# Contexts of block 0 on quadrants of TensorE, a new order for the first two units, and one buffer for what stays

## The chip, the cores and the metric

The kernel runs on one core of one Trainium2 chip. The metric is the device time of one execution in microseconds. Three runs of the kernel before took 1060.54, 1061.24 and 1062.72 us, median 1061.24 us. A further execution was recorded by the hardware profiler: it took 1059.08 us, of which the span from the first to the last instruction is 1057.3 us.

The engines are named as in the profile: PE (TensorE matmul), PEld (TensorE weight load), DVE (VectorE), ACT (ScalarE), POOL (GpSimd) and SP (SyncE, which issues the DMAs here). L12 is line 12 of the kernel before.

## The reference

The input x has 32 sequences of 64 tokens with 512 features, in float32, and each sequence has a condition vector. Two blocks follow one another. Block 0 is a conditioned RMS norm, attention with rotary positions, 8 query heads of 64 and one shared key/value head, and then a gated MLP of width 2048. Block 1 is a conditioned layer norm and an attention with 16 heads of 32, whose 4 key/value heads come from a latent of 128.

```python
def block0(x, pos, cond):                       # 8 query heads of 64, one kv head
    h = ada_rms(x, cond, ln1_w, ln1_tw)         # norm, times w * (1 + cond @ tw.T)
    q, k, v = h @ Wq.T, h @ Wk.T, h @ Wv.T      # split in heads
    q, k = rope(q, pos), rope(k, pos)
    attn = softmax(einsum('bkgsd,bktd->bkgst', q, k) / sqrt(64))
    ctx = einsum('bkgst,bktd->bkgsd', attn, v)  # the contexts that the change touches
    x = x + ctx @ Wo.T
    h = ada_rms(x, cond, ln2_w, ln2_tw)
    return x + (silu(h @ Wg.T) * (h @ Wu.T)) @ Wd.T

def block1(x, cond):                            # 16 query heads of 32, 4 kv heads
    scale, shift = split(cond @ W_ada.T + b_ada)
    h = layernorm(x) * (1 + scale) + shift
    q, c_kv = h @ Wq.T, h @ Wkd.T
    k, v = c_kv @ Wku.T, c_kv @ Wvu.T
    q, k = rope(q), rope(k)
    attn = softmax(masked(q @ k.T / sqrt(32)))
    return x + (attn @ v) @ Wo.T
```

## The kernel before

**Tiling.** The work is cut into 8 units of 256 tokens, that is, 4 sequences each. Features lie on the 128 partitions and tokens in the columns, so x of a unit is a tile of 128 x 4 x 256. For each unit there are three jobs: `attention0` (L569), `mlp` (L961) and `attention1` (L718), each a Python generator that emits a piece of the program and yields. All matmuls are in float32; the profile records each as two matmuls, and two weight loads.

**Attention of block 0.** `query` projects half of the query features into a bank of PSUM and turns them by their angles; `keys_values` does the same for the shared key and value. The values are transposed (`vt`, L643) and copied by ACT into `vblk0` (L646). `vblk0` is block-diagonal: for each sequence it holds 128 x 128, with v of 64 x 64 at top left and again at bottom right, and zeros elsewhere. The zeros are written once by POOL in `early` (L990). The scores (`sc`, L664) are computed on quadrants of the array: heads lie two to a partition tile, one in the upper and one in the lower 64 rows, so each matmul is 64 x 64. After the softmax, each half t of the unit (2 sequences) is transposed in four pieces into one bank (`pp`, L549), copied to `pT` by ACT (L550), and multiplied with the block-diagonal values:

```python
cx = abank(f"cx0_{u}_{t}").rearrange("p (b c s) -> p b c s", b=2, c=KC)
for b in range(2):                      # L681: two matmuls of 128 x 128, 256 columns
    nc.tensor.matmul(cx[:, b], vb[:, 2 * t + b].rearrange("p r d -> p (r d)"),
                     pT[:, :, b * S : (b + 1) * S], start=True, stop=True)
for b in range(2):                      # L690: two copies of 128 x 256 on ACT
    nc.scalar.copy(to[:, b], cx[:, b])
```

The contexts `cT` then go through the output projection (`output`, L553, tile `po`) and are added to x by DVE (L562). The squares of the new x (`sq_b`, ACT L489), their means (`qs_b`, L467), a root with its inverse (`r_b`), its spread over the partitions (`row_b`, L389) and the scaled `h` lead to the MLP.

**MLP.** Each of the three weight matrices is handled with seven products of half-size blocks in place of eight. A set of weights holds three loaded blocks and four sums of blocks. In the first pass the sums are made by DVE and POOL (`combine`, L243 to L246) and kept in DRAM; later passes load all seven. The tiles are `gu` (gate and up, L875) and `down` (L934).

**Order.** Engines work through their queues in order. The order of PE's pieces is set in two ways. In the start, `FIRST` (L48) is a string: letter a takes the next piece of unit 0's attention, b of unit 1's, m of the modulations 1 to 3 (products of the conditions with the modulation weights, tiles `ps_mod` and `pt_mod`). The whole stretch is kept in this order on PE by `ordered` (L96). After it, `Order.run` (L72) chooses between the MLP of a unit, the attention of block 0 of the next and of block 1 of earlier units, by the cost and latency that each piece yields. In the start and the tail `homes["now"]` lets banks be drawn from all of PSUM; in the main stage the attentions have the two banks "at". ACT, DVE, POOL and SP take their instructions as the program emits them. SP's queue holds nearly all loads, in program order: x of unit 0, the weights of the query, x of unit 1, modulation 1, `wo0`, the sets, modulations 2 and 3, and, after `FIRST`, the weights of block 1.

**Buffers.** Tensors that stay (identity, small constants, keys, values, angles, the weights of both attentions) have one tile each (`fixed`, L129). The angles of two units are computed in borrowed tiles, `p0` and `pT0` (L308). The last unit of block 1 borrows `vblk0[0]` for its values, and POOL clears it ahead of the tail (L1059).

Of the kernel before, what the change touches and what calls it, by code (L numbers as in the profile page):

```python
# [10 lines left out]
F32 = mybir.dt.float32  # L11
# [6 lines left out]
P = 128  # L18
B, S, D = 32, 64, 512
T = B * S  # L20
KC = D // P
# [23 lines left out]
TURN = (0.15911865234375, 3.628432750701904e-05, 6.4192136051133275e-09, 1.4247115856860781e-12)  # L45
ROUND = 12582912.0
WARM = 11
FIRST = "aaaaaaa bb a mm aa b a b aa bbb a b aa a bb a mmmm a bbbb".replace(" ", "")  # L48
TWO_PI = float(np.nextafter(np.float32(2 * np.pi), np.float32(0)))


# [56 lines left out]
def two_blocks(ctx: ExitStack, tc: tile.TileContext, a: dict, out: bass.AP):  # L108
# [17 lines left out]
        homes["n"] += 1  # L126
        return bank(tags[homes["n"] % len(tags)], name)

    def fixed(tag, shape, dtype=F32):  # L129
        return const.tile(shape, dtype, tag=tag, name=tag)  # L130

    def work(tag, shape, name, bufs=2):
        return wk.tile(shape, F32, tag=tag, name=name, bufs=bufs)


    ident = fixed("ident", [P, P])
    make_identity(nc, ident)
    ones = fixed("ones", [P, P])
# [6 lines left out]
    spread = fixed("spread", [P, US, P])  # L145
# [7 lines left out]
    eps0 = fixed("eps0", [P, 1])  # L153
    nc.gpsimd.memset(eps0, EPS0)
    eps1 = fixed("eps1", [P, 1])
    nc.gpsimd.memset(eps1, EPS1)
    quarter = fixed("quarter", [P, 1])
    nc.gpsimd.memset(quarter, float(np.float32(np.pi / 2)))

    positions = []  # L160
# [4 lines left out]
        positions.append(t)  # L165

    load_positions(0)
    small = fixed("small", [P, C_ALL])
# [6 lines left out]
    sign_of = small[:, C_SIGN:C_ALL]  # L175


    kblk0 = [fixed(f"kblk0{i}", [P, US, S]) for i in range(2)]

    vblk0 = [fixed(f"vblk0{i}", [P, US, 2, S]) for i in range(2)]  # L180
    vblk1 = [fixed(f"vblk1{i}", [P, US, 2, 2 * HD1]) for i in range(2)]

    s0a = fixed("s0a", [P, KC, B])
    s0b = fixed("s0b", [P, KC, B])
    s1 = fixed("s1", [P, KC, B])
    t1 = fixed("t1", [P, KC, B])
    angle = fixed("angle", [P, 2, NU * S])


    wqkv = [fixed("wqkv0", [P, KC, 384]), fixed("wqkv1", [P, KC, 256])]  # L190
    wo0 = fixed("wo0", [P, KC, D])
    wq1 = fixed("wq1", [P, KC, D])
    wkd = fixed("wkd", [P, KC, LAT])
    wkv1 = fixed("wkv1", [P, 2, P])
    wo1 = fixed("wo1", [P, KC, D])

    x_units = {}

# [109 lines left out]
    def angles(u0):  # L308

        cols = slice(u0 * S, (u0 + 2) * S)  # L310

        def some(tag, name, cols=512, bufs=2):
            return work(tag, [P, cols], f"{name}_{u0}", bufs)[:, : 2 * S]

        posi = positions.pop()
        posf, sign = some("u", "posf"), some("v", "sign")
        both = work("p0", [P, 2, 512], f"ang_lo_{u0}", 1)
        ang, lo = both[:, 0, : 2 * S], both[:, 1, : 2 * S]
        hi, prod = some("pT0", "hi", 512, 1), some("r0", "prod", UT, 1)
# [121 lines left out]
    def tile4(room, tag, name):  # L441
        return space(room, tag, KC * UT, name).rearrange("p (c t) -> p c t", t=UT)
# [126 lines left out]
    def attention0(u, room, early=None, late=None):  # L569
# [71 lines left out]
        vt = abank(f"vt_{u}").rearrange("p (b d) -> p b d", d=P)  # L641
        for b in range(US):
            nc.tensor.transpose(vt[:, b, :HD0], vT[HD0:, b].rearrange("p r s -> p (r s)"), ident[HD0:, HD0:])  # L643
        for i in range(2):
            rows = slice(i * S, (i + 1) * S)
            nc.scalar.copy(vb[rows, :, i, :], vt[rows, :, :HD0])  # L646
        yield 0.3, 4.5


# [23 lines left out]
            yield 0.5 * len(ts), 5.0 * ts[0] if lean else 10.0  # L673

        cT = tile4(room, "h", f"cT0_{u}")
        for t in range(2):
            pT = turned(ps[t], f"0_{u}_{t}", space(room, "pT", 512, f"pT0_{u}_{t}")).rearrange("p (c t) -> p c t", c=KC)
            yield 0.5, 1.2
            cx = abank(f"cx0_{u}_{t}").rearrange("p (b c s) -> p b c s", b=2, c=KC)
            for b in range(2):  # L680
                nc.tensor.matmul(  # L681
                    cx[:, b],
                    vb[:, 2 * t + b].rearrange("p r d -> p (r d)"),
                    pT[:, :, b * S : (b + 1) * S],
                    start=True,
                    stop=True,
                )
            to = cT[:, :, t * P : (t + 1) * P].rearrange("p c (b s) -> p b c s", s=S)
            for b in range(2):
                nc.scalar.copy(to[:, b], cx[:, b])  # L690
            yield 0.9, 1.5 * t
        yield from output(u, cT, wo0, f"0_{u}")


# [361 lines left out]
    def spare(tag, cols, name, bufs=2):  # L1056
        return work(tag, [P, cols], f"own_{name}", bufs)

    nc.gpsimd.memset(vblk0[0], 0.0)  # L1059
    two = [spare("h2", 1024, f"h2{i}") for i in range(2)]  # L1060
    few = spare("cs", 512, "few", 1)
    extra = spare("x", 1024, "kb6", XB)
# [5 lines left out]
        "latT": [few[:, :UT]],  # L1068
        "kr": [few[:, UT:]],
        "kb": [extra[:, :512]],  # L1070
        "pT": [extra[:, 512:], spare("pT0", 512, "pT6", 1)] * 2,
# [98 lines left out]
```

## Time and profile before

| | from | value |
|---|---|---|
| median of three runs | times | 1061.24 us |
| profiled execution | times | 1059.08 us |
| its span, first to last instruction | page | 1057.3 us |
| PE busy | page, part 1 | 1013.2 us (96%) |
| PEld busy | page, part 1 | 944.1 us (89%) |
| DVE, ACT, POOL busy | page, part 1 | 548.6, 324.5, 434.7 us |
| context matmul of block 0 (L681), 64 records | tile `cx` | 379 ns each |
| context copy of block 0 (L690), 32 | tile `cx` | 377 ns each |
| copy of values (L646), 16 | tile `vt` | 367 ns each |

A record of a matmul runs from its first to its last word through the array, so records that follow one another overlap: the distance between the starts of neighbours, not the length of one, is what it takes of PE. A line of the timeline groups such records (x4 is four records, two matmuls). The times in it count from the start of the span. What stands in square brackets is how long the engine was idle ahead of the group and what ended that.

### The profile page before, as it was taken

Reading aid. Unit: us, or ns where it says so; the run is one execution under the profiler, and the core shown is the slowest. Engines: PE = TensorE matmul, PEld = TensorE weight load, DVE = VectorE, ACT = ScalarE, POOL = GpSimd, SP = SyncE. Lnnn points to the kernel's source line nnn. Section 1 sums busy time; section 2 is a strip of 40 time slices with the busy share of each in tenths; the row PEclk is TensorE's granted clock in tenths of the full one; section 3 lists DMA queues with packets and bytes.
Section 4 is the critical chain, followed back from the end, with each engine's and each line's share of the span. In section 5 each row is a group of like instructions: output and inputs, shape, how many; then the busy total and the mean of one; then the engine's idle time right before and its main releaser. Section 6 shows DMA issues by size and latency. Waiting matters only on the chain.

```text
span 1057.3 us, 21448 instructions
## 1 busy us (share of the span) xinstructions
PE 1013.2 (96%) x8538; PEld 944.1 (89%) x8538; DVE 548.6 (52%) x1377; ACT 324.5 (31%) x682; POOL 434.7 (41%) x520
## 2 busy tenths in 40 slices
PE   7889999999999989999999998999999999999887
PEld 6779999998999989999999997999999899999765
DVE  4866646543455485343653268532755335452363
ACT  4333112344124242132422323331423422241132
POOL 4424545344255434254342543324533335432541
PEclk8989999999999999999999999999999999999899
DMA  7916896354556465662646555455735557565001
GB/s 276 328 43 219 294 312 240 136 210 151 203 210 210 143 217 177 227 222 105 224 172 221 184 182 183 150 203 203 251 118 196 173 189 284 197 230 178 11 1 40
DMA packets 68274, 198.53 MB, mean 188 GB/s; under 512 B 7248, under 2 KB 15184, under 8 KB 67792
## 3 DMA queue, kind: packets, MB, share of 16 engines
q1 hardware_dynamic: 68176, 197.17, 53.6%
q8 instruction: 68, 1.11, 0.4%
q14 instruction: 30, 0.25, 0.1%
HBM read 180.37 MB, written 16.78 MB: 186 GB/s over the span
## 4 chain that ended last, share of the span: by engine, by line
PE 79%; DVE 10%; POOL 5%; issue 2%; DMA 2%; ACT 1%; SPq 0%; ACTq 0%; POOLq 0%; DVEq 0%
PE gu L875 32%; PE down L934 16%; PE po L514 10%; PE q L514 9%; PE pp L549 2%; PE lat L514 1%; PE cx L681 1%; PE cx L845 1%; PE sc L821 1%; PE kv L514 1%; DMA set<-in_wmlp 1%; PE sc L664 1%; DVE mx L534 1%; DVE sm L542 1%; DMA x<-in_x 1%
## 5 line engine op out<-in xcount | busy, mean ns | idle before, releaser
L875 PE MATMUL gu<-h,set 128*128 128x128 f32 x2048 | 288.3, 276 | 8.9 <-DVE c L894 5.2
L875 PEld LDWEIGHTS gu<-h,set 128*128 128x128 f32 x2048 | 259.4, 192 | 15.9 <-issue 10.7
L875 PE MATMUL gu<-hc,set 128*128 128x128 f32 x1536 | 215.3, 275 | 0.0
L875 PEld LDWEIGHTS gu<-hc,set 128*128 128x128 f32 x1536 | 193.6, 192 | 0.5
L913 POOL TENSOR_TENSOR act<-c,c 128x384 f32<-128x384 f32 x64 | 66.6, 1040 | 193.6 <-DVE c L901 117.5
L934 PE MATMUL down<-td,set 128*128 128x128 f32 x1024 | 136.4, 276 | 3.2 <-POOL td L916 3.2
L934 PEld LDWEIGHTS down<-td,set 128*128 128x128 f32 x1024 | 125.1, 192 | 4.5 <-POOL td L916 4.2
L887 ACT COPY e<-gu 128x128 f32<-128x128 f32 x128 | 33.7, 265 | 279.1 <-PE gu L875 268.8
L901 DVE TENSOR_TENSOR c<-gu,u 128x256 f32<-128x256 f32 x128 | 53.4, 419 | 118.1 <-PE gu L875 117.8
L514 PE MATMUL po<-cT,wo 128*128 128x256 f32 x480 | 108.4, 380 | 2.4 <-DVE sm L542 2.1
L934 PE MATMUL down<-act,set 128*128 128x128 f32 x768 | 109.2, 278 | 0.0
L889 DVE TENSOR_TENSOR u<-e,gu 128x128 f32<-128x128 f32 x128 | 36.1, 282 | 130.4 <-ACT e L887 129.8
L514 PEld LDWEIGHTS po<-cT,wo 128*128 128x128 f32 x480 | 89.3, 190 | 14.2 <-ACT cT L854 2.6
L934 PEld LDWEIGHTS down<-act,set 128*128 128x128 f32 x768 | 97.9, 192 | 4.2 <-issue 2.4
L544 POOL TENSOR_TENSOR p<-p,sm 128x512 f32<-128x512 f32 x40 | 41.3, 1052 | 116.5 <-DVE sm L543 110.6
L525 POOL TENSOR_TENSOR qT<-u_q,v_q 128x512 f32<-128x512 f32 x30 | 38.1, 1270 | 93.8 <-DVE v_q L524 93.8
L562 DVE TENSOR_TENSOR x<-x,po 128x512 f32<-128x512 f32 x32 | 22.0, 687 | 75.9 <-PE po L514 75.9
L970 ACT ACT_TABLE_LOAD x34 | 43.6, 1283 | 55.8 <-DVE c L901 55.4
L514 PE MATMUL q<-h,wqkv 128*128 128x256 f32 x256 | 58.4, 380 | 0.0
L514 PE MATMUL q<-h,wq 128*128 128x256 f32 x224 | 52.1, 385 | 1.6 <-POOL h L750 1.6
L514 PEld LDWEIGHTS q<-h,wqkv 128*128 128x128 f32 x256 | 47.7, 191 | 6.4 <-issue 0.4
L915 POOL TENSOR_TENSOR td<-act 128x256 f32<-128x256 f32 x64 | 47.6, 744 | 10.0 <-DVE act L912 3.8
(276 smaller groups left out, 1407.4 us busy)
## 6 DMA issues: line engine op xcount, KB each, us to landing
set<-sums SPq DMA_DIRECT2D x168, 512.0 KB, 5.8
set<-in_wmlp SPq DMA_DIRECT2D x192, 384.0 KB, 4.7
sums<-set SPq DMA_DIRECT2D x24, 512.0 KB, 4.7
x<-in_x SPq DMA_DIRECT2D x8, 512.0 KB, 5.7
out_x<-x SPq DMA_DIRECT2D x16, 256.0 KB, 2.1
mod<-in_mod SPq DMA_DIRECT2D x7, 512.0 KB, 6.2
a<-in_wmlp SPq DMA_DIRECT2D x24, 128.0 KB, 4.3
wo<-in_wo SPq DMA_DIRECT2D x2, 1024.0 KB, 8.4
```

Source lines behind the costliest of these rows:

```text
L514: nc.tensor.matmul(ps, w[:, k, cols], h[:, k, :], start=(k == 0), stop=(k == KC - 1))
L525: nc.gpsimd.tensor_tensor(dst, u, v, ALU.add)
L544: nc.gpsimd.tensor_tensor(p8, p8, sm.unsqueeze(2).to_broadcast(wide), ALU.mult)
L562: nc.vector.tensor_tensor(x[:, part], x[:, part], po, ALU.add)
L875: nc.tensor.matmul(ps, w[:, slot, k * P : (k + 1) * P], b[of][:, k], start=start and k == 0, stop=k == 1, skip_group_check=True)
L887: nc.scalar.copy(e, ps[:, 0])
L889: nc.vector.tensor_tensor(u2, e, ps[:, 1], ALU.add)
L901: nc.vector.tensor_tensor(c.rearrange("p (a b) t -> p a b t", b=2)[:, :, 1], ps[:, 2:4], u2.unsqueeze(1).to_broadcast([P, 2, HT]), ALU.add,)
L913: nc.gpsimd.tensor_tensor(act[:, 1:4], gate[:, 1:4], c[:, 1:4], ALU.mult)
L915: nc.gpsimd.tensor_tensor(td[:, 0:2], act[:, 1:3], act[:, 0:2], ALU.subtract)
L934: nc.tensor.matmul(sums_of[u][p][:, c], w[:, slot, c * P : (c + 1) * P], b[of], start=q % NP == 0 and i % 2 == 0 and c == 0, stop=q % NP = ...
L970: nc.scalar.activation(gate[2][:, 0], gate[0][:, 0], AF.Silu)
```

## The change

**Contexts on quadrants.** `vblk0` keeps its 4 x 64 columns of values, once in the upper and once in the lower 64 partitions, with no zeros. A context is now 64 x 64 times 256 columns: row half r by the parity of the head, column half b by the sequence. The results of row half r go to a bank of their own, and ACT copies each quadrant. Units 0 and 1 (the "lean" ones) do this for each half t, with 4 matmuls and 4 copies of 64 x 256; units 2 to 7 do both halves together after both transposes, with 8 matmuls and 4 copies of 64 x 512. The values are copied by one ACT instruction instead of two, and two of the four early memsets fall away. The yields that the planner reads change with it.

**FIRST.** The string of the first two units is another. The pieces on PE up to the first scores are as before. After that the order, with one entry per piece, is:

```
before: q0_1_0 pp_0_0 tab_1,row_1 cx0_0_0 pp_0_1 q0_1_1 cx0_0_1 vt_1 po_0_0 po_0_1 sc0_1_0 sc0_1_1
        qs_b0 ps_mod2 pt_mod2 ps_mod3 pt_mod3 row_b0 pp_1_0 cx0_1_0 pp_1_1 gu cx0_1_1 gu po_1 ...
after:  q0_1_0 tab_1,row_1 pp_0_0 q0_1_1 cx0_0_0 pp_0_1 vt_1 ps_mod2 pt_mod2 cx0_0_1 sc0_1_0 sc0_1_1
        po_0_0 po_0_1 ps_mod3 pp_1_0 qs_b0 cx0_1_0 pt_mod3 pp_1_1 row_b0 cx0_1_1 gu po_1 ...
```

Each modulation piece also issues loads on SP's queue, so that loads of modulation 2 come ahead of `wo0` there, and the sets 3 and 4 behind it.

**Buffers.** All tensors that stay are slices of one tile, "stays", of 14103 columns. The angles have tiles of their own, `ang0` to `ang2`; `pT0` has two buffers; the last unit's values lie in a spare buffer of `pT1`.

```diff
+STAY = 14103
-FIRST = "aaaaaaa bb a mm aa b a b aa bbb a b aa a bb a mmmm a bbbb".replace(" ", "")
+FIRST = "aaaaaaa bb a mm aa bb a bbb aa b mm a bb aa a m b a b m b a b".replace(" ", "")
...
-    def fixed(tag, shape, dtype=F32):
-        return const.tile(shape, dtype, tag=tag, name=tag)
+    stays = {"all": const.tile([P, STAY], F32, tag="stays", name="stays"), "at": 0}
+
+    def fixed(shape):
+        n, i = int(np.prod(shape[1:])), stays["at"]
+        stays["at"] += n
+        assert stays["at"] <= STAY
+        t = stays["all"][:, i : i + n]
...
-    vblk0 = [fixed(f"vblk0{i}", [P, US, 2, S]) for i in range(2)]
+    vblk0 = [fixed([P, US, HD0]) for i in range(2)]
...
-        both = work("p0", [P, 2, 512], f"ang_lo_{u0}", 1)
-        ang, lo = both[:, 0, : 2 * S], both[:, 1, : 2 * S]
-        hi, prod = some("pT0", "hi", 512, 1), some("r0", "prod", UT, 1)
+        ang, lo, hi = (some(f"ang{i}", f"ang{i}", 2 * S, 1) for i in range(3))
+        prod = some("r0", "prod", UT, 1)
...
-    RING = {"h": 2, "p1": 2, "pT1": 2}
+    RING = {"h": 2, "p1": 2, "pT0": 2, "pT1": 2}
...
-        for i in range(2):
-            rows = slice(i * S, (i + 1) * S)
-            nc.scalar.copy(vb[rows, :, i, :], vt[rows, :, :HD0])
+        nc.scalar.copy(vb, vt[:, :, :HD0])
...
+        pTs = []
+
+        def contexts(ts):
+
+            banks = [abank(f"cx0_{u}_{ts[0]}_{r}").rearrange("p (t c s) -> p t c s", t=2, c=KC) for r in range(2)]
+            for i, t in enumerate(ts):
+                for b in range(2):
+                    for r, cx in enumerate(banks):
+                        rows = slice(r * S, (r + 1) * S)
+                        nc.tensor.matmul(
+                            cx[b * HD0 : (b + 1) * HD0, i],
+                            vb[rows, 2 * t + b],
+                            pTs[t][rows, :, b * S : (b + 1) * S],
+                            start=True,
+                            stop=True,
+                        )
+            by_two = cT.rearrange("p c (t b s) -> p t c b s", b=2, s=S)[:, ts[0] : ts[-1] + 1]
+            for r, cx in enumerate(banks):
+                for b in range(2):
+                    nc.scalar.copy(by_two[r * HD0 : (r + 1) * HD0, :, :, b], cx[b * HD0 : (b + 1) * HD0, : len(ts)])
+
         for t in range(2):
...
-            cx = abank(f"cx0_{u}_{t}").rearrange("p (b c s) -> p b c s", b=2, c=KC)
...
-            for b in range(2):
-                nc.scalar.copy(to[:, b], cx[:, b])
-            yield 0.9, 1.5 * t
+            if lean:
+                contexts([t])
+                yield 0.6, 1.5 * t
+        if not lean:
+            contexts([0, 1])
+            yield 1.1, 2.5
...
-        for z in (*vblk0, *vblk1):
+        for z in vblk1:
             nc.gpsimd.memset(z, 0.0)
...
-    nc.gpsimd.memset(vblk0[0], 0.0)
+    zeros = spare("pT1", 512, "vb7", 2).rearrange("p (b r d) -> p b r d", b=US, r=2)
+    nc.gpsimd.memset(zeros, 0.0)
...
-        "vb": vblk0[0],
+        "vb": zeros,
```

More of the change, by code (lines that the diff above doesn't have):

```diff
@@ L127, in abank @@
         return bank(tags[homes["n"] % len(tags)], name)
-    def fixed(tag, shape, dtype=F32):
-        return const.tile(shape, dtype, tag=tag, name=tag)
+    stays = {"all": const.tile([P, STAY], F32, tag="stays", name="stays"), "at": 0}
[4 more added lines that the diff above has]
+        t = stays["all"][:, i : i + n]
+        if len(shape) == 2:
+            return t
+        names = "abc"[: len(shape) - 1]
+        return t.rearrange(f"p ({' '.join(names)}) -> p {' '.join(names)}", **dict(zip(names, shape[1:])))
     def work(tag, shape, name, bufs=2):
         return wk.tile(shape, F32, tag=tag, name=name, bufs=bufs)
-    ident = fixed("ident", [P, P])
+    ident = fixed([P, P])
     make_identity(nc, ident)
-    ones = fixed("ones", [P, P])
+    ones = fixed([P, P])
     nc.gpsimd.memset(ones, 1.0 / D)
@@ L143, in two_blocks @@
         nc.tensor.matmul(idle[:, :P], ones, ones, start=True, stop=True)
-    spread = fixed("spread", [P, US, P])
+    spread = fixed([P, US, P])
     nc.gpsimd.memset(spread, 0.0)
@@ L152, in two_blocks @@
             nc.gpsimd.tensor_copy(to, block.to_broadcast([HALF0, 2, 2, HALF1]))
-    eps0 = fixed("eps0", [P, 1])
+    eps0 = fixed([P, 1])
     nc.gpsimd.memset(eps0, EPS0)
-    eps1 = fixed("eps1", [P, 1])
+    eps1 = fixed([P, 1])
     nc.gpsimd.memset(eps1, EPS1)
-    quarter = fixed("quarter", [P, 1])
+    quarter = fixed([P, 1])
     nc.gpsimd.memset(quarter, float(np.float32(np.pi / 2)))
@@ L167, in two_blocks @@
     load_positions(0)
-    small = fixed("small", [P, C_ALL])
+    small = fixed([P, C_ALL])
     nc.sync.dma_start(small, a["small"])
@@ L175, in two_blocks @@
     sign_of = small[:, C_SIGN:C_ALL]
-    kblk0 = [fixed(f"kblk0{i}", [P, US, S]) for i in range(2)]
-    vblk0 = [fixed(f"vblk0{i}", [P, US, 2, S]) for i in range(2)]
[L181 to L195, printed above, removed]
+    kblk0 = [fixed([P, US, S]) for i in range(2)]
+    vblk0 = [fixed([P, US, HD0]) for i in range(2)]
+    vblk1 = [fixed([P, US, 2, 2 * HD1]) for i in range(2)]
+    s0a = fixed([P, KC, B])
+    s0b = fixed([P, KC, B])
+    s1 = fixed([P, KC, B])
+    t1 = fixed([P, KC, B])
+    angle = fixed([P, 2, NU * S])
+    wqkv = [fixed([P, KC, 384]), fixed([P, KC, 256])]
+    wo0 = fixed([P, KC, D])
+    wq1 = fixed([P, KC, D])
+    wkd = fixed([P, KC, LAT])
+    wkv1 = fixed([P, 2, P])
+    wo1 = fixed([P, KC, D])
     x_units = {}
@@ L675, in attention0 @@
         cT = tile4(room, "h", f"cT0_{u}")
+        pTs = []
[16 more added lines that the diff above has]
+                    nc.scalar.copy(by_two[r * HD0 : (r + 1) * HD0, :, :, b], cx[b * HD0 : (b + 1) * HD0, : len(ts)])
         for t in range(2):
-            pT = turned(ps[t], f"0_{u}_{t}", space(room, "pT", 512, f"pT0_{u}_{t}")).rearrange("p (c t) -> p c t", c=KC)
+            pT = turned(ps[t], f"0_{u}_{t}", space(room, "pT", 512, f"pT0_{u}_{t}"))
+            pTs.append(pT.rearrange("p (c t) -> p c t", c=KC))
             yield 0.5, 1.2
-            cx = abank(f"cx0_{u}_{t}").rearrange("p (b c s) -> p b c s", b=2, c=KC)
-            for b in range(2):
[L681 to L690, printed above, removed]
-            yield 0.9, 1.5 * t
+            if lean:
[4 more added lines that the diff above has]
+            yield 1.1, 2.5
         yield from output(u, cT, wo0, f"0_{u}")
@@ L1070, in two_blocks @@
         "kb": [extra[:, :512]],
-        "pT": [extra[:, 512:], spare("pT0", 512, "pT6", 1)] * 2,
+        "pT": [extra[:, 512:], spare("pT0", 512, "pT6", 2)] * 2,
     }
```

## The prediction

> **What bounds the kernel now.** I read the page's busy table and clock row first, then busy time by stretch, then PE's timeline at the contexts and in the start.
>
> ```profile
> span 1057.3 us, 21448 instructions
> PE 1013.2 (96%) x8538; PEld 944.1 (89%) x8538; DVE 548.6 (52%) x1377; ACT 324.5 (31%) x682; POOL 434.7 (41%) x520
> ```
>
> PE is the bound. The stretches (us, then busy time of PE, PEld, DVE, ACT, POOL with counts, PE's clock, DMA share, GB/s) show where it idles:
>
> ```profile
> 0.00:75.00 75.00, 61.07 (x595) 51.44 (x596) 50.67 (x136) 28.61 (x62) 29.91 (x48) 0.89 0.63 228
> 75.00:978.00 903.00, 888.14 (x7457) 841.12 (x7456) 460.79 (x1163) 274.38 (x569) 374.84 (x442) 1.00 0.58 199
> 978.00:1057.30 79.30, 63.99 (x490) 51.52 (x488) 37.17 (x80) 21.47 (x51) 29.97 (x30) 0.96 0.05 17
> ```
>
> Idle: 13.9 us in the start, 14.9 in the long middle, 15.3 in the tail. So the middle shortens only by less PE work, the start by less waiting too. PE's timeline at the places that matter (start, length, line, tile, records):
>
> ```profile
> 205.84 1.15 PE L664 MATMUL sc<-kblk,qT 64*64 64x64 f32 x32
> 206.92 0.71 PE L875 MATMUL gu<-hc,set 128*128 128x128 f32 x4
> ...
> 223.43 1.03 PE L681 MATMUL cx<-pT,vblk 128*128 128x256 f32 x4
> 224.29 0.60 PE L549 MATMUL pp<-ident,p 128*128 128x128 f32 x4
> ...
> 323.47 1.16 PE L664 MATMUL sc<-kblk,qT 64*64 64x64 f32 x64
> 324.56 0.71 PE L934 MATMUL down<-act,set 128*128 128x128 f32 x4
> ```
>
> Start to next start: a context half takes 224.29 - 223.43 = 0.86 us, 0.215 per record. The 64 quadrant records of the scores take 1.09 us when emitted together; where the scheduler split them by row half, 32 take 1.08. So four quadrants run at once if they stand together in PE's order, two otherwise.
>
> The start, where order decides:
>
> ```profile
> 47.36 7.17 PE L514 MATMUL po<-cT,wo 128*128 128x256 f32 x32 [0.35 <-ACT cT L690]
> 54.47 1.16 PE L664 MATMUL sc<-kblk,qT 64*64 64x64 f32 x64
> 56.47 0.65 PE L467 MATMUL qs_b<-sq_b,ones 128*32 128x64 f32 x32 [0.84 <-ACT sq_b L489]
> ...
> 60.73 0.33 PE L295 MATMUL pt_mod<-ident,rows 128*128 128x128 f32 x1 [2.73 <-DVE rows L292]
> ...
> 66.23 2.07 PE L681 MATMUL cx<-pT,vblk 128*128 128x256 f32 x4 [0.68 <-ACT pT L550]
> ...
> 68.95 1.06 PE L875 MATMUL gu<-h,set 128*128 128x128 f32 x4
> ...
> 70.65 1.71 PE L681 MATMUL cx<-pT,vblk 128*128 128x256 f32 x4
> ```
>
> The second unit's scores come after the 7.1 us of `po`, so its softmax is in the open: PE waits, its clock falls to 0.68 in 60 to 65 us and 0.50 in 65 to 70, and contexts take 1.5 to 1.7 us.
>
> **What the Trainium skill says.** "TensorE: Matmul & The Clock Gate", The mechanism: matmuls on different tiles of the array overlap, while they finish in order. The trace agrees: 64 in 1.09 us against 32 in 1.08. "TensorEngine Tiling (Array Packing)", Key Properties: a change of tiling mode drains TensorE. With 16 records of 64 columns per quadrant at a quarter of 0.215 us, 0.85 us streams; 1.09 - 0.85 = 0.24 us is what the trace shows beside it, 0.16 at the block-1 contexts (239.84 - 238.83 = 1.01 us for 8 records two at a time, 0.85). I take 0.17. The same page, PSUM Bottleneck: tiling doesn't speed evacuation. Agreed: the 64x256 copy of the values takes 0.367 us, the 128x256 copy of the contexts 0.377. The Clock Gate page, What's actually happening: TensorE's clock is halved after an idle window of about 3.4 us; the 0.50 above fits.
>
> **The change part by part.**
>
> *Contexts, units 2 to 7.* Before: 8 records, 8 x 0.215 = about 1.74 us per unit. After: 16 records of 256 columns, four at once: 16 x 0.213 / 4 = 0.85, and 0.17 for the switch: 1.02, so -0.72. The built program's order on PE has them so in units 3, 5, 6, 7: -2.9. In unit 2 part stands split (0.60 + 1.03): -0.1. In unit 4 they go row half by row half: 2 x 1.02 against 1.74, +0.3. One group of block-1 scores comes apart: +0.17. Sum -2.5 us. Bounds: all two at a time, 6 x 0.3 = +1.8; all at once, -4.3.
>
> *Copies.* Before, two of 0.377 after the last context. After, four of 128x512's duration (0.589, the `pT` copy): 2.36 us between contexts and `po`. PE has other matmuls in that gap by the planner's order: 2.45 us in unit 2, 4.8, 2.7, 2.7, 4.8 and 3.7 in units 3 to 7, at 0.223 per matmul. So about covered, with ACT sometimes busy first (a silu, 0.8) and one query waiting for a bank: +0.4 in all. Uncovered it would be up to 2 us a unit. ACT's sum grows by 6 x (2.36 - 1.51) plus the start's 4 x 0.7, less eight value copies of 0.367: about +5 us on an engine 31% busy, nothing.
>
> *The start.* By hand, from the durations above. Tables, the first `pp`, the query and both contexts' first half end at 43.1 (the lean contexts cost 0.60 for 0.88). The values' transpose waits for DVE to about 45; `ps_mod2` to 46.2; `pt_mod2`, in PE's order ahead of the second contexts, waits for DVE's `rows` (behind the keys and rope of unit 1) to 48.8, and the contexts, scores and `po` are queued behind it; contexts to 49.7; scores of unit 1 to 50.8, while four ACT copies run. `po` 51.35 to 58.5: 4 us later than before. But under it DVE, ACT and POOL do unit 1's softmax. Then x (0.69), `sq_b` (1.06), means at 61.05, a table load (1.28) and root 63.9, inverse 64.3, `row_b` 65.2, `h` (1.3): first `gu` at 66.5 with no contexts left, against 68.95 with 1.5 us of contexts left: 2.45 + 1.5 = 3.95, and 0.25 off for a later `hc` on DVE: -3.7 us. The removed memsets (0.53 each on POOL) lie under the loads. The moved loads: `wo0` is issued near 28 instead of 20.5 us and lands in 8.4, before its use at 51; sets 3 and 4 come up to 1 us later, and the DMA share is 0.00 to 0.02 from 60 to 75 us, so they have room. Bounds: 0 to -8 (with full clock, next part).
>
> *Buffers.* Slices begin at any 4 bytes. No row shows such a weight load. The nearest, L514's, takes 190 ns against 215 of matmul, so 10% more would hide; I take 0, at most +1. More buffers for angles: no DVE time saved on a path, 0. The late memset of `vblk0[0]` blocked POOL for 5.2 us at 712 with no PE idle there: 0.
>
> Sum: -3.7 - 2.5 + 0.4 = -5.8 against 1059.1, so a profiled execution of 1053.3. The median stands 2.2 above the profiled one: 1055.5.
>
> **Rivals.**
>
> *A: the start gives nothing.* `po` 4 us later is 4 us lost if x, `sq_b`, root and `row_b` are the whole path and ACT's queue (the softmax exponent with its table load, `pT` and context copies, all between) delays `sq_b` by the same. For it: ACT is in order and `sq_b` stands behind them. Against: exponents are due by 55, before `po` ends. Then -2.1 alone: 1059.1.
>
> *B: no throttle.* With the softmax hidden, PE's gaps from 58 to 66 us stay short, the clock stays at 1, and the 7 us that now run at half speed save about 4 more: 1051.5. Against: the path above still leaves gaps of 1 to 1.5 us in a row.
>
> *C: slower, by evacuation.* `po` waits for the copies. If ACT's queue puts a table load and a silu (1.28 + 0.8) ahead of them, or the copies of 64 partitions with two strides cost more than 0.59, the cover of 2.5 us is gone. At 2.0 us in each of 6 units, 12 instead of 0.4: -5.8 + 11.6 = +5.8, 1067. It decides from about 1 us per unit, where it equals the gain. Against: ACT's 31%, and copies of that size at 0.589 in the page.
>
> *D: quadrants don't do as they say.* Pairs that share a row half follow each other, and only two run at once everywhere: 2.04 for 1.02 in four units, +4.1: 1059.6. The scores at 323 speak against it.
>
> **How the numbers follow.** Forecast 0.50 (1053 to 1058), A 0.17, B 0.15, C 0.08, D 0.10. A measurement of this kernel tells about 0.2%, 2.1 us, from no change. Faster: the forecast, B, half of A, a third of D: 0.77. Same: the rest of A and half of D, 0.12. Slower: C and the rest of D, 0.11. The range from 1049.5 to 1062 leaves out C, the far end of B and little of D: under 0.2. It holds the bounds: -4.3 - 8 is outside, but needs both extremes.
>
> **What would show it.** Context groups of 8 matmuls (16 records) with 1.0 us to their neighbour, and 2.0 in unit 4; four ACT copies of 0.59; PE's idle before `po` for `cT` under 0.5 us per unit; in the start `po` at about 51.4, first `gu` near 66.5, and no context after 66; idle in the middle still near 15 us. Wrong: idle before `po` named for `cT` of over 1 us (C), first `gu` after 69 (A), a clock of 1.0 from 60 to 70 (B), a context group of 2 us in every unit (D).

## The result and the profile after

Seven runs of the changed kernel took 1054.20 to 1058.84 us, median 1056.37, against 1061.24 (1060.36 to 1064.04, seven runs): ratio 0.994, interval 0.9923 to 0.9956. That is 4.9 us between the medians, 6.4 us by the ratio. The forecast was 1055.5, in a range of 1049.5 to 1062. The profiled execution took 1055.26 us, 3.8 under that of before.

The page's span and busy table, and busy time by the stretches that the prediction used (columns as there):

```profile
span 1053.4 us, 21591 instructions
...
PE 1012.6 (96%) x8602; PEld 938.7 (89%) x8602; DVE 546.7 (52%) x1377; ACT 329.1 (31%) x680; POOL 432.8 (41%) x518
```

```profile
0.00:75.00 75.00, 61.26 (x617) 50.43 (x618) 49.26 (x133) 29.87 (x67) 29.08 (x46) 0.89 0.63 228
75.00:978.00 903.00, 890.07 (x7521) 839.30 (x7521) 460.92 (x1167) 277.82 (x562) 376.30 (x446) 1.00 0.57 200
```

PE's busy total fell by only 0.6 us, and the first 75 us hold as much idle as before (13.7 for 13.9 us). So the fixed stretches hide where the time went, and I cut both traces at the same work instead, below.

The groups themselves are what was forecast. PE's timeline of the changed kernel at the contexts of units 3 and 4:

```profile
341.78 0.61 PE L899 MATMUL gu<-h,set 128*128 128x128 f32 x4
342.32 1.09 PE L694 MATMUL cx<-pT,stays 64*64 64x256 f32 x16
343.34 0.71 PE L958 MATMUL down<-act,set 128*128 128x128 f32 x4
343.89 0.28 PE L958 MATMUL down<-td,set 128*128 128x128 f32 x1
...
467.64 1.08 PE L694 MATMUL cx<-pT,stays 64*64 64x256 f32 x8
468.65 0.71 PE L958 MATMUL down<-act,set 128*128 128x128 f32 x4
469.30 1.08 PE L694 MATMUL cx<-pT,stays 64*64 64x256 f32 x8
470.31 0.71 PE L958 MATMUL down<-act,set 128*128 128x128 f32 x4
```

Start to next start, 1.02 us for 16 records together, 1.01 for 8 that share a row half, so 2.02 in unit 4: within 0.02 us of the forecast.

But a group of quadrants also makes its neighbours longer, and its own length doesn't show that. In unit 3 the four `gu` records ahead of it take 342.32 - 341.78 = 0.54 us, and the four `down` records behind it 343.89 - 343.34 = 0.55. In the kernel before, the contexts use the whole array, 128x128, as their neighbours do, and four `gu` ahead of them take 226.96 - 226.51 = 0.45:

```profile
226.51 0.61 PE L875 MATMUL gu<-hc,set 128*128 128x128 f32 x4
226.96 1.03 PE L681 MATMUL cx<-pT,vblk 128*128 128x256 f32 x4
```

That is 0.1 us on each side of a group. In unit 4 the four `down` between the two groups pay twice: 469.30 - 468.65 = 0.65.

The start of the changed kernel (the lines that answer to those of before):

```profile
50.39 0.33 PE L307 MATMUL pt_mod<-stays,rows 128*128 128x128 f32 x1 [2.57 <-DVE rows L304]
50.64 0.69 PE L694 MATMUL cx<-pT,stays 64*64 64x256 f32 x8
51.13 1.91 PE L673 MATMUL sc<-stays,qT 64*64 64x64 f32 x64
52.97 7.95 PE L525 MATMUL po<-cT,stays 128*128 128x256 f32 x32
...
66.71 1.08 PE L400 MATMUL row_b<-r_b,stays 128*128 128x64 f32 x8 [1.80 <-DVE r_b L471]
68.03 1.00 PE L694 MATMUL cx<-pT,stays 64*64 64x256 f32 x8 [0.24 <-ACT pT L561]
69.18 2.08 PE L899 MATMUL gu<-h,set 128*128 128x128 f32 x8
```

The wait for the transpose of modulation 2, ahead of the contexts and `po`, is there (2.57 us), and the wait of 2.73 us at 60.73 is gone. The first `gu` comes at 69.18, no earlier than before (68.95), but with no contexts left after it.

Cut at the same work, counted in PE's timeline (the first score; the first, 201st, 361st and last record of the `down` products; the end), all kernels of this study have these stretches in us. The names are those of the experiments below. A star marks a last-but-one stretch that holds one window of 3.4 us at half clock, two stars two. Each row is a single execution. Those of `old_order`, `order_v2` and `double_copies` are the slowest of their kernel, 5.4 to 6.2 us above its median.

| kernel | to first score | to first `down` | first pass, to 201st | to 361st | middle, to last | to end |
|---|---|---|---|---|---|---|
| before | 31.6 | 56.6 | 69.9 | 90.2 | 736.0 | 73.0 |
| changed | 33.6 | 53.6 | 72.1 | 90.8 | 730.1 | 73.1 |
| after_again | 32.9 | 53.7 | 74.0 | 90.8 | 731.7* | 73.1 |
| aligned | 32.2 | 53.6 | 73.7 | 90.8 | 731.6* | 73.2 |
| no_stays | 32.9 | 54.9 | 73.4 | 90.8 | 729.7 | 73.3 |
| contexts_only | 32.7 | 58.5 | 69.9 | 90.8 | 729.7 | 73.3 |
| old_order | 34.5 | 60.4 | 73.9 | 90.9 | 731.9* | 73.2 |
| order_only | 32.8 | 53.9 | 71.4 | 90.2 | 737.9* | 73.3 |
| placed | 33.5 | 58.1 | 70.5 | 90.2 | 732.9* | 74.0 |
| no_kept | 32.1 | 54.8 | 71.0 | 90.8 | 731.3* | 73.4 |
| order_v2 | 34.1 | 52.9 | 73.5 | 90.8 | 731.3* | 74.2 |
| order_v3 | 31.4 | 52.1 | 73.7 | 90.8 | 731.7* | 73.3 |
| v3_quads | 33.7 | 52.8 | 73.1 | 91.9 | 730.9* | 69.9 |
| double_copies | 32.6 | 55.2 | 74.3 | 91.5 | 736.2** | 74.0 |

From this table: the reordered part of the start became 3.0 us shorter. But 2.0 us were lost ahead of the first score, where the order of PE did not change, and 2.2 in the first pass over the sets. The stretch to the 361st, in which PE never stands idle in either kernel, became 0.6 us longer. It holds the contexts of unit 2 in two groups: they take 1.59 us in place of 1.74, but their neighbours 0.4 more, and a group of block 1's contexts 0.3 more. The middle became 5.9 us shorter, nearly three times the forecast's 2.1.

### The profile page after: what moved, and what is told of

It reads as the page before. It is cut to its first block, busy times and chain, and to the rows that moved or that the text cites. A ratio compares the mean times of both kernels' runs of the same rounds, so it can differ in the third digit from the quotient of the medians.

```text
span 1053.4 us, 21591 instructions
## 1 busy us (share of the span) xinstructions
PE 1012.6 (96%) x8602; PEld 938.7 (89%) x8602; DVE 546.7 (52%) x1377; ACT 329.1 (31%) x680; POOL 432.8 (41%) x518
## 4 chain that ended last, share of the span: by engine, by line
PE 81%; DVE 8%; POOL 5%; DMA 2%; issue 2%; ACT 1%; SPq 0%; ACTq 0%; POOLq 0%; DVEq 0%
PE gu L899 34%; PE down L958 17%; PE po L525 10%; PE q L525 9%; DMA set<-in_wmlp 2%; PE cx L869 2%; PE sc L845 1%; PE lat L525 1%; PE pp L560 1%; PE sc L673 1%; PE kv L525 1%; PE cx L694 1%; DVE sm L553 1%; PE tab L400 1%; DVE mx L545 1%
## 5 line engine op out<-in xcount | busy, mean ns | idle before, releaser
L899 PEld LDWEIGHTS gu<-h,set 128*128 128x128 f32 x2048 | 258.8, 192 | 15.5 <-issue 10.4
L911 ACT COPY e<-gu 128x128 f32<-128x128 f32 x128 | 33.7, 264 | 259.9 <-PE gu L899 246.8
L525 PE MATMUL q<-h,stays 128*128 128x256 f32 x480 | 111.3, 385 | 1.5 <-POOL h L774 1.5
L525 PE MATMUL po<-cT,stays 128*128 128x256 f32 x480 | 109.0, 382 | 2.1 <-DVE sm L553 2.1
L525 PEld LDWEIGHTS q<-h,stays 128*128 128x128 f32 x480 | 90.9, 193 | 14.3 <-POOL h L774 1.7
L525 PEld LDWEIGHTS po<-cT,stays 128*128 128x128 f32 x480 | 89.8, 191 | 14.0 <-ACT cT L878 2.6
L994 ACT ACTIVATE c<-gu 128x128 f32<-128x128 f32 x64 | 17.7, 277 | 90.2 <-DVE c L925 82.2
```

What stands on the lines that cost most here:

```text
L525: nc.tensor.matmul(ps, w[:, k, cols], h[:, k, :], start=(k == 0), stop=(k == KC - 1))
L899: nc.tensor.matmul(ps, w[:, slot, k * P : (k + 1) * P], b[of][:, k], start=start and k == 0, stop=k == 1, skip_group_check=True)
L911: nc.scalar.copy(e, ps[:, 0])
L994: nc.scalar.activation(gate[2][:, 0], gate[0][:, 0], AF.Silu)
```

## The experiments

All are set against runs of the kernel before on the same chip. Those had medians of 1063.92, 1062.67 and 1063.12 us in the three sets, so ratios are compared and not medians of different sets.

**First set: the parts alone.** `contexts_only` is the kernel before with the quadrants and what comes with them, the later place of the contexts and a second buffer for `pT0`:

```diff
 # changed kernel, less the string, the one buffer and the angles' tiles
-FIRST = "aaaaaaa bb a mm aa bb a bbb aa b mm a bb aa a m a b m b a b".replace(" ", "")
+FIRST = "aaaaaaa bb a mm aa b a b aa bbb a b aa a bb a mmmm a bbbb".replace(" ", "")
...
-        t = stays["all"][:, i : i + n]
+        return const.tile(shape, F32, tag=f"fix{count['n']}", name=f"fix{count['n']}")
...
-        ang, lo, hi = (some(f"ang{i}", f"ang{i}", 2 * S, 1) for i in range(3))
+        both = work("p0", [P, 2, 512], f"ang_lo_{u0}", 1)
```

> The kernel before with the quadrant contexts (half-size values, the last unit's values in a spare buffer) and nothing else: old order of the first two units, one tile per tensor that stays, angles in borrowed tiles. The traces of the two kernels lie -3.1 us apart between the first and the last MLP down product. If all of that is the contexts and the order of the first units is worth nothing in the end (theory T), 3 to 4 us under the kernel before, near 1058 us, with context groups of 1.0 us and no idle of PE for cT ahead of po. If the record is right (forecast F), 2.1 us, 1059 us.

Measured 1058.12 us (1055.1 to 1061.2), ratio 0.9945 (0.9927 to 0.9963): 5.8 us under the kernel before, more than either theory said. In the middle it is 6.3 us shorter, and no `po` there waits for `cT`. In the start the quadrants cost time with the old order, as PE's timeline of this kernel shows:

```profile
48.80 7.17 PE L520 MATMUL po<-cT,fix 128*128 128x256 f32 x32 [1.22 <-ACT cT L699]
...
62.16 0.33 PE L301 MATMUL pt_mod<-fix,rows 128*128 128x128 f32 x1 [2.73 <-DVE rows L298]
...
71.10 1.13 PE L689 MATMUL cx<-pT,fix 64*64 64x256 f32 x8 [1.17 <-ACT pT L556]
```

Four copies where there were two: `po` waits 1.22 us for `cT` (0.35 before), and the last contexts 1.17 us for a `pT` copy that stands behind four others on ACT.

`order_only` is the kernel before with the new string:

```diff
-FIRST = "aaaaaaa bb a mm aa b a b aa bbb a b aa a bb a mmmm a bbbb".replace(" ", "")
+FIRST = "aaaaaaa bb a mm aa bb a bbb aa b mm a bb aa a m a b m b a b".replace(" ", "")
```

> The kernel before with the new string for the first two units alone. F: 3.7 us faster, 1057.5 us. T: the new order ends the start 1 to 3 us earlier at the first down product, and the first pass over the sets of weights, with the DMA engines 0.9 busy, takes it back by 145 us: within 1 us of the kernel before. Rival: 2 us of the changed kernel's loss ahead of the first scores come from its one buffer or its angles; then these first 34 us are as in the kernel before here.

Measured 1061.22 us (1059.3 to 1062.6), ratio 0.9974 (0.9963 to 0.9986): 2.8 us faster, between the two. The trace has the reordered start shorter by 2.7 us and the first pass longer by 1.4. Its first score comes at 32.8 us with the old buffers and angles, so what was lost ahead of it is not theirs alone.

`old_order` is the changed kernel with the old string (the lines of the last diff, exchanged).

> The changed kernel with the old string of the first two units. F: 3.7 us slower than the changed kernel, 1060. T: within 1 us of the changed kernel, 1056 to 1057. If buffers matter, it differs from the contexts alone.

Measured 1060.67 us (1056.8 to 1066.5), ratio 0.9975 (0.9963 to 0.9987). Against the changed kernel's 0.994 that is 0.35%, 3.7 us: F's number. But `contexts_only`, with the same old order, was at 0.9945. These two differ in the one buffer and the angles' own tiles; the buffer costs nothing with the new order (next), so either the angles do harm in the old order or the spread of the start is behind it. No run here separates them.

`no_stays` is the changed kernel with a tile for each tensor (the second hunk of the first diff).

> The changed kernel with one tile for each tensor that stays in place of the one buffer; all else as changed. F and T: no difference from the changed kernel, 1056.4 us within 1 us. If slices at any 4 bytes cost time (late small loads, slower weight loads), 1 to 2 us faster than the changed kernel, and first scores at 31.6 us in place of 33.6.

Measured 1056.37 us (1054.8 to 1057.9), ratio 0.9925 (0.9913 to 0.9938).

**Second set: buffer, start, first pass.** `after_again` is the changed kernel itself.

> The changed kernel unaltered, to stand on the same chip as the others. Single runs of one kernel lie up to 8 us apart, and the traces so far show it to arise ahead of 90 us: the first down product comes at 86.7 to 94.8 us in six profiles, while the time from 250 us to the last one is the same for kernels with the same middle. So 4.9 us under the kernel before as measured, and over the kernel with separate tiles by 0 (buffer costs nothing) or by 2.5 us (it does: contexts alone 1058.1 against 1060.7 with the buffer and angles added, both with the old order).

Measured 1056.89 us (1053.9 to 1058.3), ratio 0.9943 (0.9925 to 0.996): the result again, 5.8 us between medians. `aligned` starts each slice at a multiple of 64 bytes:

```diff
-        stays["at"] += n
+        stays["at"] += -(-n // 16) * 16
```

> The changed kernel, with each slice of the one buffer starting at a multiple of 16 columns (64 bytes). If slices off such a line cost time, as the kernel with separate tiles: 2.5 us under the changed kernel. If one tile for all costs it (waits on the whole), as the changed kernel. If neither costs anything, all three are alike.

Measured 1056.7 us (1052.8 to 1058.0), ratio 0.9936 (0.9917 to 0.9955). The three agree within their intervals, and the weight loads of the output projections show no difference. First the group of the changed kernel, then of `aligned` (busy, mean ns, idle ahead):

```profile
L525 PEld LDWEIGHTS po<-cT,stays 128*128 128x128 f32 x480 | 89.8, 191 | 14.0 <-ACT cT L878 2.6
```

```profile
L525 PEld LDWEIGHTS po<-cT,stays 128*128 128x128 f32 x480 | 89.5, 191 | 13.8 <-ACT cT L878 2.5
```

191 ns a load in both. Slices at any 4 bytes cost nothing here.

`order_v2` moves the transpose of modulation 2 behind unit 0's projection:

```diff
-FIRST = "aaaaaaa bb a mm aa bb a bbb aa b mm a bb aa a m a b m b a b".replace(" ", "")
+FIRST = "aaaaaaa bb a mm aa bb a bbb aa b m a bb aa m a m a b m b a b".replace(" ", "")
```

> The changed kernel with the transpose of modulation 2 moved behind the first unit's output projection, where nothing waits for it. The trace shows PE idle 2.57 us for it, with the contexts, scores and projection queued behind. Theory D (the order's gain is lost to this wait): first down product 2.5 us earlier, 84.7 us for 87.2, and the time 2.5 us lower. Theory S (the first pass over the sets is bound by DMA and takes any gain of the start back): first down product as early, but the time at 250 us unchanged.

Measured 1052.39 us, ratio 0.9911 (0.9888 to 0.9934): five of six runs lie at 1050.9 to 1054.4, the profiled one at 1058.6. It is 10 us under the kernel before and 4.5 under the changed kernel beside it, the fastest of this study. Its interval overlaps that of `after_again` (0.9925 to 0.9934). The reordered start in its profile is 0.8 us shorter than in `after_again`, not 2.5:

```profile
49.87 0.76 PE L694 MATMUL cx<-pT,stays 64*64 64x256 f32 x8 [1.53 <-ACT pT L561]
...
52.21 7.17 PE L525 MATMUL po<-cT,stays 128*128 128x256 f32 x32 [0.65 <-ACT cT L704]
```

With the wait for `rows` gone, the contexts wait 1.53 us for a `pT` copy and `po` 0.65 us for `cT`. The five faster runs had a mean granted clock of 0.989 to 0.993, `after_again` 0.985 to 0.988; so part of the gain may be a clock less often halved, which its profile, taken of its slowest run (0.982), cannot show. An estimate: over the 180 executions of this study, one is 0.6 us faster for each 0.001 of mean clock than others of its kernel (correlation -0.78), so the 0.0038 between the means goes with about 2.4 of the 4.5 us.

`no_kept` leaves out the writes of the first pass:

```diff
-                nc.sync.dma_start(t[:, 0:4], kept[i])
+                nc.sync.dma_start(t[:, 0:4], a["wmlp"][i])
...
-        if q < NP:
-            nc.sync.dma_start(kept[3 * (q % NP) + m], sets[n][:, 0:4])
```

> The changed kernel without the writes of the sums of the first pass to DRAM; later passes load blocks of the weights in their place, as many bytes, so the MLP of all later passes is other than the reference's. 12.6 MB less for the DMA engines between 35 and 160 us. S: PE's idle of 2.4 us between 100 and 150 us goes, the time falls by 2 to 3 us. D: the pass is bound by PE and DVE, the idle for DVE stays, and the time moves by less than 1 us.

Measured 1055.71 us (1054.1 to 1057.2), ratio 0.9934 (0.9916 to 0.9952), 1.2 us under `after_again`: between the two theories, and within the intervals. Busy time from 88 to 160 us, first of the changed kernel, then of `no_kept`; the last numbers are the clock, the DMA engines' share and GB/s:

```profile
88.00:160.00 72.00, 69.56 (x634) 68.14 (x633) 41.91 (x120) 12.51 (x33) 34.12 (x46) 1.00 0.86 285
```

```profile
88.00:160.00 72.00, 70.77 (x643) 69.45 (x644) 47.58 (x124) 12.84 (x33) 33.36 (x46) 1.00 0.56 172
```

With the share down from 0.86 to 0.56, PE idles 1.2 us less. The first pass takes 71.0 us, where the changed kernel and its equals (`after_again`, `aligned`, `no_stays`) took 72.1 to 74.0. In the changed kernel DVE's sums of blocks wait 17.5 us there for loads of sets (from 87 to 159.3 us), and a `down` waits 0.5 us for such a sum; in `no_kept` DVE waits 8.9 us, and no `down` waits for a sum. In the kernel before no `down` waits for a sum either, though DVE waits 16.4 us for loads. Leaving out the writes to DRAM takes 1 to 3 us off the first pass in these traces, and 1.2 off the median. So not all of the loss is explained. `no_kept` also lets a set's buffer be loaded again without waiting for the write, so load on the engines and that wait are not told apart. And `old_order`, whose first `down` comes last of all (94.8 us), has a first pass of 73.9 us too, so an early start alone is not what makes it long.

**Third set: what the middle gained.** `placed` keeps the old matmuls and copies, and emits them where the change does, with the change's second buffer for `pT0`:

```diff
-    RING = {"h": 2, "p1": 2, "pT1": 2}
+    RING = {"h": 2, "p1": 2, "pT0": 2, "pT1": 2}
...
             yield 0.5, 1.2
-            cx = abank(f"cx0_{u}_{t}").rearrange("p (b c s) -> p b c s", b=2, c=KC)
...
-            yield 0.9, 1.5 * t
+            if lean:
+                context(t, pT)
+                yield 0.9, 1.5 * t
+        if not lean:
+            for t in range(2):
+                context(t, pTs[t])
+            yield 1.1, 2.5
```

> The kernel before with its own context matmuls and copies (block-diagonal values, 128x128), but emitted where the change emits them, both halves together after both transposes and with the change's yield, so that PE's order in the middle is that of the changed kernel. In the traces the stretch from the 361st record of the down products to the last one takes 736.0 us before and 730.1 after, of which 14.4 and 10.5 are idle of PE; the context groups account for 3.2 of it. If the placing does the rest: idle near 10.5, stretch near 733, the time 2.5 to 3 us under the kernel before. If the faster contexts themselves do it (buffers free earlier): idle stays at 14.4 and the time as before.

Measured 1058.31 us (1052.3 to 1061.6), ratio 0.9955 (0.994 to 0.9971): 4.8 us faster with not one matmul cheaper. PE's idle in the middle fell from 14.4 to 10.3 us, as in the changed kernel (10.5). The waits from 250 to 985 us that make the difference, first before, then `placed` (us in total, times, longest):

```profile
PE gu L875 <- DVE c L894: 3.5, 3, 1.8
PE pp L549 <- POOL p L544: 3.2, 2, 2.5
PE down L934 <- POOL td L916: 3.2, 5, 1.2
PE gu L875 <- ACT c L970: 1.9, 2, 1.7
```

```profile
PE gu L885 <- DVE c L904: 3.2, 3, 1.8
PE down L944 <- POOL td L926: 2.5, 5, 1.2
PE pp L549 <- POOL p L544: 1.9, 1, 1.9
...
PE gu L885 <- ACT c L980: 0.2, 1, 0.2
```

They are not waits for contexts, but of `gu` for ACT, `pp` for POOL and `down` for POOL, which another order of pieces meets or doesn't. Less the starred window (1.6 us, see the end), the middle is 731.3 us: 4.7 of the 5.9 us are the placing with its buffer, which were not taken apart, and 1.2 to 1.6 are left for the quadrants. From 250 us on their groups take 6.1 us against 8.7 in `placed`. About half of these 2.6 us comes back, and not as idle time, which is alike (10.5 and 10.3): six groups with 0.2 us on their neighbours are 1.2. Less the 0.6 us that the stretch to the 361st lost (90.8 against 90.2 in `placed`), the quadrants are worth 0.6 to 1.0 us. The runs can't tell that from nothing: `contexts_only` is 0.1% under `placed`, within the intervals.

`order_v3` changes `order_v2` once more, so that unit 1's keys come behind unit 0's first contexts on ACT:

```diff
-FIRST = "aaaaaaa bb a mm aa bb a bbb aa b m a bb aa m a m a b m b a b".replace(" ", "")
+FIRST = "aaaaaaa bb a mm aa bb a b aa bb b m a bb aa m a m a b m b a b".replace(" ", "")
```

> The changed kernel with the transpose of modulation 2 behind the projection (order_v2, 1052.4 us), and unit 1's keys and second query behind unit 0's first contexts. In order_v2 the second contexts wait 1.53 us for the copy of their pT, which stands on ACT behind a copy of unit 1's keys that waits for DVE, and the first contexts' copies. If that order of ACT is the cause, the wait goes, some 0.7 us for the first pT copy comes, and the time is 0.5 to 1 us under order_v2: 1051.5. If the first pass over the sets takes all further gain, 1052.4 again.

Measured 1055.09 us (1053.7 to 1059.5), ratio 0.9933 (0.9915 to 0.9951), no better than `order_v2`. The two waits of `order_v2` are gone, and there are others, as PE's timeline of this kernel says:

```profile
40.06 0.66 PE L694 MATMUL cx<-pT,stays 64*64 64x256 f32 x8 [0.67 <-ACT pT L561]
49.96 0.93 PE L673 MATMUL sc<-stays,qT 64*64 64x64 f32 x48 [1.29 <-POOL qT L536]
```

The second query, now later, makes the scores wait for POOL. The reordered start is 0.8 us shorter than in `order_v2`; that the time isn't is left open.

`v3_quads` holds scores and contexts in the order emitted, in `order_v3`:

```diff
+        together = nullcontext if lean else lambda: ordered(tc, mybir.EngineType.PE)
...
+            with together():
                 for n in range(KC * len(ts)):
```

> order_v3 with the scores and contexts of units 2 to 7 held in the order in which they are emitted, so that the four quadrants stand together on PE; only the first matmul of a group can stand apart, waiting for the second bank. Groups split by row half now: contexts of unit 4 (2.02 us), unit 2 (1.59), scores of unit 2 (2.16), 5, 6 and 7 (1.72 to 1.90). Whole ones take 1.02 and 1.09, the lone first one some 0.3: 0.7 + 0.3 + 0.8 + 3 x 0.4 = 3.0 us under order_v3 if nothing waits for the second bank; no gain or a loss if PE then stands still for it.

Measured 1057.45 us (1054.1 to 1062.6), ratio 0.9951 (0.9931 to 0.9971): no gain. The groups do stand together (14 of 16 context records of unit 4 in 1.02 us, the first two apart for 0.57), and PE stands still elsewhere for it:

```profile
217.71 0.44 PE L560 MATMUL pp<-stays,p 128*128 128x128 f32 x2 [1.66 <-POOL p L555]
```

With the scores tied together, a transpose of unit 2 comes to stand earlier on PE, 7.6 us after the last score with its wait, instead of 10.6 without one in `order_v3`, ahead of what POOL has yet to finish. Another order of pieces brought another wait, as in `placed` it took some away.

`double_copies` does each context copy of units 2 to 7 twice:

```diff
+                    for _ in range(1 if lean else 2):
                         nc.scalar.copy(by_two[r * HD0 : (r + 1) * HD0, :, :, b], cx[b * HD0 : (b + 1) * HD0, : len(ts)])
```

> The changed kernel with every context copy of units 2 to 7 done twice: 4.7 us between contexts and projection in place of 2.35. By the cover that the record counts (2.45, 1.3 to 4.8, 2.7, 2.7, 4.8, 3.7 us): waits of 2.2, 0 to 3, 2, 2, 0 and 1, 7 us slower, with PE's idle ahead of the projection named for cT. If the cover is larger than counted, less than 2 us slower; rival C would then be far from deciding.

Measured 1060.17 us (1057.7 to 1065.6), ratio 0.9971 (0.9958 to 0.9984): 3.0 us slower than `after_again` by the ratios, between the two expectations. PE's waits name the copies with 3.0 us:

```profile
PE po L525 <- ACT cT L705: 2.4, 4, 1.2
...
PE q L525 <- ACT cT L705: 0.6, 1, 0.6
```

So 2.35 us more in each of six units, 14 us on ACT, show as 3. The cover was larger than counted, and a single set of copies is hidden.

## Why the prediction was right, and where only its sum was

The time and the sign were right: -5.8 us forecast, -4.9 and -5.8 between medians in two sets. That the sum was right is luck, by errors that cancel: in the traces the middle with the stretch before it gained 5.3 us where 2.1 were forecast, and the start with the first pass lost 1.2 where 3.7 were to be gained.

*Contexts, units 2 to 7.* Right in every group after (1.02, 2.02 and 1.59 us). Before they took 11.0 us in the trace, not 6 x 1.74 = 10.4, in part by waits of 0.2 us that end two of the groups; so the groups shrank by 3.3 us, 0.6 of it by the placing alone (10.4 in `placed`). The step that was mis-sized is "0.17 for the switch". The 0.17 us lie inside a group, and it measures 0.2 us more on the neighbours, 1.6 us in eight groups. The prediction's own lines had half of it: the 0.71 us of the four records behind the scores, where 0.61 is usual. So the quadrants gave 0.6 to 1.0 us, not 2.5.

*The term that was missing.* The step that failed is "So the middle shortens only by less PE work": the sum counted only the groups. That the new yields and the later contexts also move every other piece, and that this removes 4 us of waits, mostly for ACT and POOL, stood nowhere in it. `placed` shows 4.7 us by this, with the second buffer. Its sign "idle in the middle still near 15 us" failed: it is 12.9 us from 75 to 978. The gain was not to be read from the cost of any instruction; it could have been bounded, by the 14.9 us of idle that the middle had.

*Copies.* The duration was right (0.577 us in the tile's row for 0.589). The 0.4 us of waiting did not come: no `po` of the middle waits for `cT`. Rival C is far off: `double_copies` costs 3.0 us with twice the copies, where C assumed 12 with one set.

*The start.* The mechanism was right (softmax under `po`, a wait for `rows` ahead of it), and the reordered part shrank by 3.0 us for a forecast of 3.7; `po` came at 52.97, not 51.35, mostly for the 2.0 us lost ahead of the first score, and took 7.95 us for 7.17, as a window at half clock fell on it (51.2 to 54.6 us, behind the wait for `rows`); the first `gu` came at 69.18, not 66.5. The step that failed is the silent one, that what the start gains stays gained. The first pass takes 2.2 us longer in this trace, and 1.4 in `order_only`; `no_kept`, with the writes left out, gives back 1 to 3 in its trace and 1.2 in the median. The prediction had looked at the DMA share from 60 to 75 us (0.00) and not at 100 to 150 (0.9). By ratios the order is worth 0.2 to 3.7 us (before to `order_only` 2.8, `contexts_only` to `no_stays` 2.1 and to `after_again` 0.2, `old_order` to changed 3.7). `order_only` alone, with an interval clear of 1, shows that it is not lost whole; how much of it adds to the quadrants stays open.

*The rivals.* A was right in its effect in the profiled run (the start gave nothing, and its sign, a first `gu` after 69, came) and had the cause in a small part only: `sq_b` waited for x, not for ACT, but the root's table load stood 0.9 us behind a `pT` copy and `sq_a` (64.37 us, the means done by 63.5). B came in part: half clock in 60 to 75 us fell from 10.2 us to 3.4 (0.82 and 0.84 from 65 to 75), but the window on `po` is new. D is excluded by the groups.

*Buffers at nothing.* Right: `no_stays`, `aligned` and `after_again` agree.

*The offset of 2.2 us* between profiled execution and median was 1.1 us for the changed kernel. It is no constant but the luck of one start.

## What to carry to other kernels

Where a planner places pieces by their stated cost, an edit's own instructions can be its smaller part: count the idle time that another order could remove or add, and keep the old instructions at the new places as a test. A group that cuts the array into other tiles than its neighbours is to be priced with its neighbours, here 0.2 us more. A gain in a start can be lost in the next stretch; look at what that one waits for, here in part sums whose loads share the DMA engines (0.9 busy) with the writes. Compare traces by landmarks in the work rather than at fixed times, since one early delay shifts everything behind it.

## What the hardware showed that was not expected

The clock is halved in windows of 3.4 us, and in the middle one such window is what separates the two executions of the changed kernel. Busy time of the changed kernel and of `after_again` from 254 to 260 us, with the clock as the third number from the end:

```profile
254.00:260.00 6.00, 6.00 (x57) 6.00 (x56) 4.10 (x9) 1.35 (x4) 2.66 (x5) 1.00 0.52 210
```

```profile
254.00:260.00 6.00, 5.62 (x36) 5.62 (x37) 2.04 (x2) 1.04 (x3) 3.92 (x6) 0.72 0.73 276
```

Both follow the same idle of 1.93 us, as PE's timelines show:

```profile
253.13 0.44 PE L560 MATMUL pp<-stays,p 128*128 128x128 f32 x2 [1.93 <-POOL p L555]
```

```profile
254.38 0.44 PE L560 MATMUL pp<-stays,p 128*128 128x128 f32 x2 [1.93 <-POOL p L555]
```

One was halved, the other not, and their middles differ by 731.7 - 730.1 = 1.6 us and no more. So an idle gap of about 2 us costs itself, and at times 1.6 us on top.

The traces also show when. In each of them the halved windows start at whole multiples of 3.413 us from one another (in `after_again` at 9.6, 50.6, 67.6 and 255.4 us). The gap of `after_again` fell whole into the window ahead of the halved one, 252.0 to 255.4; that of the changed kernel fell into two, with 1.34 and 0.59 us. In the middles of all kernels 11 windows are halved, each behind a window with 1.92 to 2.61 us of idle; no other window has over 1.91, but for one with 1.93 in the kernel before. This agrees with what the Trainium skill says in "TensorE: Matmul & The Clock Gate", What's actually happening, of a window of some 3.4 us that runs free of the program. It does not agree that the window has to be idle throughout, as the prediction took it: 1.9 of its 3.4 us were enough, and in the start of the kernel before, where the clock fell to 0.50, PE was never idle for more than 2.73 us in a row.

A product of 128x64 on DVE took 0.21 us in one place and 1.12 in another of the changed kernel, the second while POOL worked on `h`. DVE, then POOL:

```profile
12.72 1.12 DVE L395 TENSOR_TENSOR stays<-few 128x64 f32<-128x64 f32 x1 [0.99 <-ACT few L394]
...
14.50 0.21 DVE L395 TENSOR_TENSOR stays<-few 128x64 f32<-128x64 f32 x1
```

```profile
11.71 2.05 POOL L508 TENSOR_TENSOR h<-x,stays 128x512 f32<-128x512 f32 x2 [6.42 <-DVE stays L311]
```

In the kernel before, POOL's second half waited 0.41 us for x and the slow product fell behind DVE's half of `h`; here it fell ahead of it, and the first projection came 0.9 us later (14.64 for 13.71). It is half of what was lost ahead of the first score; a second query that ran under a halved clock (4.6 us for 3.5) is the other half. The slow product ends at 13.84 us, just after POOL's work (13.76). That the two engines hinder each other there is read from the times alone; no run tested it.
